# Waits by tile, unread matrix products and an earlier square root in the stages ahead of a recurrence

## The chip, the cores and the metric

The kernel runs on one core of a Trainium2 chip. The metric is the device time of one launch in microseconds (us), as the median of several runs. Beside it there is one profiled execution, whose trace gives every instruction's start and length. Engines are named as the profile names them: PE (matrix products; PEld its weight loads), DVE (vector), ACT (scalar, with function tables), POOL (GpSimd), SP (which issues transfers). SBUF is the on-chip memory, PSUM the eight banks that PE writes.

## What is computed

The input x is one image of 256 by 256 points with 32 channels. Four layers follow each other, and each adds its result to x. `_gn` normalises over the whole image in 16 groups of two channels, so no layer can begin its work on the values before the one ahead has made its last value.

```python
# layer 0; _L0_conv_ref, called with _gn(x)
mn = (m - mu) * rsqrt(var + LN_EPS) * ln_gamma + ln_beta     # over the 32 channels
v = mn @ Wv
g = sigmoid(mn @ Wg)
a = softmax(einsum('bsihc,btihc->bstih', q, k) * C**-0.5, axis=2)
o = g * einsum('bstih,bsihc->bsihc', a, v)
x = x + (o.reshape(B, s, i, H * C) @ Wo + bo)

# layers 1 and 2: 3x3 mean, the two Sobel gradients, their length
x = x + sqrt(grad_x**2 + grad_y**2 + 1e-6)                   # of pooled _gn(x)

# layer 3: two stacked recurrent cells over 256 steps, 256 sequences
x = x + recurrence(_gn(x), W_lat, W_cell, gn_gamma, gn_beta, W_out, ...)
```

In layer 0 the softmax runs over t, but v in the second einsum has the index s. So the weights a sum to one and drop out: o = g * v. Neither q nor k is computed.

## The kernel before

**Layout.** Partition (j, c) holds channel c of column 4*b + j, the free axis holds the 256 rows s, and b = 0..63 are blocks of four columns. `pair(t, k)` is two blocks, 128 x 512 values; k runs over 32 pairs (`NST`). `xa` and `xb` are the two copies of the image, 64 KB per partition each.

**Order.** The front, the Sobel layers and the recurrence are written under a manual schedule: on each engine the instructions run in the order in which the Python code emits them. The attention, the Sobel body and the recurrence emit from lists of (time, operation) that are sorted by their planned time. An engine whose next instruction has to wait holds up everything behind it.

**Load (L147 to L254).** Ten pieces of columns, `nats`, come by two DMAs each on SP's queue: two half pieces, six whole ones, two half ones. Per pair PE turns the data with `transpose` into a PSUM bank `pt` (seven of them), ACT copies it to `xa` (L250), and DVE takes BN_STATS (L251). After the pieces SP issues the constants `kg`, the weights `wone` (W_v, W_g), gamma, beta, the recurrence's norm parameters `gb`, `kt` and `wc`. `busy_here(n)` emits n products of `ident` with itself into a bank `warm` that nobody reads: seven at the start, three after each of the first two pieces. The last ACT instruction is a `table` call, which makes ACT load the table that has the square root.

**Group norm of layer 0 (L266 to L319).** DVE aggregates the statistics (L267), PE averages over the groups (`pm`, L276), DVE makes `less` (minus the mean), `d` and `q`, PE averages again (`pv`, L284), ACT takes the root `gstd`, DVE its reciprocal `scale` and the scaled centring matrix `cen` (L314). `busy_ln(5)` are five unread products ahead of `pm`. Behind `pv` on PE stand four products for the biases (L288), one for the test whether the recurrence's norm is plain (`total_same`, L790), and two that centre the weights (L300); ACT copies the former into `wbias` and scales the latter into `wv4` and `wg4`. `shifted(k)` writes xb = xa + less for pair k, on DVE, but for pair 2, which ACT does (L303). `compare` and `decide` are DVE's part of the test; the flag that they make is read by SP (L750).

**Layer norm (L321 to L397).** For g = 0..7, the groups of four pairs, PE makes 16 centred products of 32 rows (L366) into four banks, ACT squares them (L390), and PE sums the squares over the channels into a variance bank (L347, issued one group late). The variance of group 0 gives `rstds[0]`, that of the others `rstds[1]`. The first is taken inside the loop:

```python
for j, pc in enumerate(pcs):
    if g == EARLY + 1 and j == 1:          # EARLY = 1
        std = deviations()                 # ACT, L357
        nc.vector.reciprocal(rstds[0], std)   # DVE, L380
        for k in range(3):
            rowsets[k] = rows_of(k)        # SP, L328: 4 transfers per pair
        for k in range(5 * J, NST):
            shifted(k)                     # DVE: pairs 20..31
        ...
        for k in range(3):
            scaled(k)                      # L338: xb *= rows; DVE for k=0, POOL else
    nc.scalar.activation(sqs[-1], pc, AF.Square)
```

Pairs 4 to 19 are shifted by a loop that is emitted at g = 0, after that group's products.

**Attention (L399 to L529).** Per pair and half: PE makes g and v (L459), ACT the sigmoid (`sg`, L468), DVE (v + bias) * sg (L472), PE the projection (L485), ACT and POOL the sum into `xa` (L500, L501), DVE BN_STATS (L504). The products of pair k need `scaled(k)`. Pairs from 3 on have their rows transferred and are scaled in between.

**Sobel layer (L543 to L739), run twice.** `shift` is the group norm: aggregate, `busy(before)`, `pm`, `busy(2)`, two constants on ACT, `d`, `q`, `pv`, `busy(after)`; before is 3 and after is 16. `busy` are unread products of `ident` with `kg`. Then per pair: `convert` (ACT), `twos` and `threes` (DVE), `ends` (ACT), `fours`, `smooth` (DVE for pairs 0 and 1, POOL else), `difference` (POOL), `mixed(k, 1)` on the differences and `mixed(k, 0)` on the smoothed rows (PE, L670), `square` of each (ACT, L676), `total` (DVE, L680), `root` (ACT), `residual` and `statistics` (DVE). A mixed product (k, which) takes blocks up to the first of pair k + 1, which only its last part reads. Rows of `dh` and `sh` in the trace are the differences and the smoothed values.

**Pools.** Tiles come from pools. By default a pool that takes over the memory of closed pools waits, at its first use, for everything that was done with them. Only the pool `keep` has `reuse_waits="tile"`, by which each tile waits just for the users of the memory that it lies on.

Of the kernel before, what the change touches and what calls it, by code (L numbers as in the profile page):

```python
# [11 lines left out]
F32 = mybir.dt.float32  # L12
BF16 = mybir.dt.bfloat16
AF = mybir.ActivationFunctionType
ALU = mybir.AluOpType
AX = mybir.AxisListType
PSUM = bass.MemoryType.PSUM
# [6 lines left out]
P = 128  # L24
H = 128
L = 2
D = 256
# [34 lines left out]
def net_kernel(  # L62
# [20 lines left out]
    nc = tc.nc  # L83
# [6 lines left out]
    second = ExitStack()  # L90
# [23 lines left out]
        return t  # L114

    one = eps_tile(1.0, "one")
    wv4 = big2.tile([P, D], F32, name="wv4")
    wg4 = big2.tile([P, D], F32, name="wg4")
    bo4 = per_channel(b_o, "bo4")
    bout4 = per_channel(b_out, "bout4")  # L120

# [60 lines left out]
    def pair(t, k):  # L182
        return t[:, 2 * k : 2 * k + 2, :].rearrange("p b s -> p (b s)")
# [8 lines left out]
    with tc.tile_pool(name="nat", bufs=6, side="right") as natp, tc.tile_pool(  # L192
        name="ps_in", bufs=7, space=PSUM
    ) as ps_in:
        nats = []
        for wl in WIDTHS:
            name, bufs = ("nat", 6) if wl == 32 else ("half", 4)
            nat = natp.tile([P, 2, wl, C], F32, name=name, bufs=bufs)
            nats.append((nat, w0, wl))
            for h in range(2):  # L200
                nc.sync.dma_start(out=nat[:, h], in_=x_nat[:, h, w0 : w0 + wl, :])
            w0 += wl
        nc.sync.dma_start(out=kg, in_=consts[:, 0:2, :])
        for t, v in (
            (wone[0], w_v),
            (wone[1], w_g),
            (gamma, ln_gamma.rearrange("(c o) -> c o", o=1)),
            (beta, ln_beta.rearrange("(c o) -> c o", o=1)),
        ):
            nc.sync.dma_start(out=t, in_=v)  # L210
        count = mp.tile([1, 1], F32, name="count")
        compare, total_same, decide = norm_test(tc, mp, count, gn_gamma, gn_beta)
        nc.sync.dma_start(out=kt, in_=consts[:, 3:NK, :])
        rw = RecurrentWeights(tc, cells, one, w_cell, b_cell)
        reduces, subtractions = rw.centring()
        wgam = []
        for w in wone:
            wgam.append(mp.tile([C, D], F32, name="wgam", bufs=2))
            nc.gpsimd.tensor_scalar(wgam[-1], w, gamma, None, ALU.mult)
        cen4 = mp.tile([C, J, C], F32, name="cen4")  # L220
        nc.gpsimd.tensor_copy(
            cen4, kg[0:C, K_CEN, 0:C].unsqueeze(1).to_broadcast([C, J, C])
        )
        mean_of = mp.tile([P, J], F32, name="mean_of")
        nc.gpsimd.tensor_sub(mean_of, ident[:, 0:P:C], kg[:, K_CEN, 0:P:C])
        nc.gpsimd.memset(avg, 0.0)
        for g in range(GROUPS):
            nc.gpsimd.tensor_copy(avg[:, g, g, :], mean_of)

        warm = ps_in.tile([P, P], F32, name="warm", bufs=1)  # L230

        def busy_here(n):
            for _ in range(n):
                nc.tensor.matmul(warm, lhsT=ident, rhs=ident, start=True, stop=True)

        busy_here(7)
        for i, (nat, w0, wl) in enumerate(nats):
            for b2 in range(wl // (2 * J)):
                pt = ps_in.tile([P, 2, 2, P], F32, name="pt")
                for b in range(2):  # L240
                    for h in range(2):
                        lo = (b2 * 2 + b) * J
                        nc.tensor.transpose(
                            pt[:, b, h, :],
                            nat[:, h, lo : lo + J, :].rearrange("p w c -> p (w c)"),
                            ident,
                        )
                blk = w0 // J + b2 * 2
                dst = xa[:, blk : blk + 2, :].rearrange("p b s -> p (b s)")
                nc.scalar.copy(dst, pt.rearrange("p b h s -> p (b h s)"))  # L250
                nc.vector.bn_stats(stats[:, blk // 2, :], dst)  # L251
            if i < 2:
                busy_here(3)
        table(AF.Sqrt, xa[:, NB - 1, 0:1])  # L254

    big3 = second.enter_context(tc.tile_pool(name="big3", bufs=1, side="right"))
    xb = big3.tile([P, NB, S], F32, name="xb")
    cen = mp.tile([P, P], F32, name="cen")

    psums = ExitStack()  # L260
    ps_at = psums.enter_context(tc.tile_pool(name="ps_at", bufs=1, space=PSUM))

    def bank(n):
        return ps_at.tile([P, 2 * S], F32, name="pa", tag=f"bank{n}")
# [5 lines left out]
    def busy_ln(n):  # L270
        for _ in range(n):
            nc.tensor.matmul(junk[:, 0:S], lhsT=ident, rhs=kg, start=True, stop=True)

    busy_ln(5)
    pm = bank(1)[:, 0:1]
    nc.tensor.matmul(pm, lhsT=kg[:, K_GN, :], rhs=mv[:, 0:1], start=True, stop=True)  # L276
    less = small.tile([P, 1], F32, name="less")
    nc.vector.tensor_scalar_mul(less, pm, -1.0)
    d = small.tile([P, 1], F32, name="d")
# [2 lines left out]
    nc.vector.scalar_tensor_tensor(q, d, d, mv[:, 1:2], ALU.mult, ALU.add)  # L282
    pv = bank(2)[:, 0:1]
    nc.tensor.matmul(pv, lhsT=kg[:, K_GN, :], rhs=q, start=True, stop=True)  # L284
    pbias = bank(3)
    for i, w in enumerate(wone):
        for half in range(2):
            nc.tensor.matmul(  # L288
                pbias[:, 2 * i + half : 2 * i + half + 1],
                lhsT=w[:, half * P : (half + 1) * P],  # L290
                rhs=beta,
                start=True,
                stop=True,
            )
    compare()
    psame = bank(6)[0:1, 0:1]
    total_same(psame)
    pws = [bank(4 + i)[:, 0:D] for i in range(2)]
    for pw, w in zip(pws, wgam):
        nc.tensor.matmul(  # L300
            pw, lhsT=cen4.rearrange("c j k -> c (j k)"), rhs=w, start=True, stop=True
        )
    nc.scalar.activation(pair(xb, 2), pair(xa, 2), AF.Identity, bias=less)  # L303
    gstd = small.tile([P, 1], F32, name="gstd")
    nc.scalar.activation(gstd, pv, AF.Sqrt, bias=gn_eps)

    def shifted(k):
        nc.vector.tensor_scalar(pair(xb, k), pair(xa, k), one, less, ALU.mult, ALU.add)

    shifted(0)  # L310
    shifted(1)
    scale = small.tile([P, 1], F32, name="scale")
    nc.vector.reciprocal(scale, gstd)
    nc.vector.tensor_scalar(cen, kg[:, K_CEN, :], scale, None, ALU.mult)  # L314
    shifted(3)
    decide(psame, flag)
    nc.scalar.copy(wbias, pbias[:, 0:4].rearrange("p (i h) -> p i h", i=2))
    for w, pw in zip((wv4, wg4), pws):
        nc.scalar.activation(w, pw, AF.Copy, scale=scale)  # L319

    EARLY = 1  # L321
    rstds = [lnp.tile([P, 2 * S], F32, name=f"rstd{i}") for i in range(2)]
# [14 lines left out]
        e = nc.gpsimd if k else nc.vector  # L337
        e.tensor_mul(pair(xb, k), pair(xb, k), rowsets.pop(k))  # L338

    with tc.tile_pool(name="lnq", bufs=9) as lnq:  # L340
        pvars = []

        def variance(g, sqs):
# [17 lines left out]
        for g in range(GROUPS):  # L361
# [13 lines left out]
                    shifted(k)  # L375
            sqs = []
            for j, pc in enumerate(pcs):
                if g == EARLY + 1 and j == 1:
                    std = deviations()
                    nc.vector.reciprocal(rstds[0], std)  # L380
                    for k in range(3):
                        rowsets[k] = rows_of(k)
                    for k in range(5 * J, NST):
                        shifted(k)
                    for f in reduces:
                        f()
                    for k in range(3):
                        scaled(k)
                sqs.append(lnq.tile([P, 2 * S], F32, name="sq"))
                nc.scalar.activation(sqs[-1], pc, AF.Square)  # L390
# [46 lines left out]
        (20.2213, "r", 0, 0),  # L437
        (22.5883, "bn", 0, 0),
    ]
    with tc.tile_pool(name="at", bufs=3) as atp:  # L440
        free = [4, 5, 6, 0, 1, 2, 3, 7]
        held, sbuf = {}, {}
        slots = {name: list(range(n)) for name, n in (("sg", 10), ("o", 11))}
# [10 lines left out]
        def one_of(o, u, j, k):  # L454
            bias = lambda i: wbias[:, i, u : u + 1]
            if o in ("v", "g"):
                rows = slice(j * C, (j + 1) * C)
                w = wv4 if o == "v" else wg4
                nc.tensor.matmul(  # L459
                    take((o, u, j, k)),  # L460
                    lhsT=w[rows, u * P : (u + 1) * P],
                    rhs=pair(xb, k)[rows],
                    start=True,
                    stop=True,
# [65 lines left out]
    psums.close()  # L530
    front.close()
    lns.close()
    lw = ctx.enter_context(tc.tile_pool(name="lw", bufs=1))
    rw.rest(tc, lw, ident, bout4, w_lat, b_lat, w_out)


# [6 lines left out]
    def sobel_layer(src, dst, moments, before, after, between):  # L543

        stats = new_stats()
        stack = ExitStack()
        kp = stack.enter_context(tc.tile_pool(name="sobk", bufs=1))
        sp = stack.enter_context(tc.tile_pool(name="sob", bufs=2))
        ps_s = stack.enter_context(tc.tile_pool(name="ps_s", bufs=3, space=PSUM))
        ps_c = stack.enter_context(tc.tile_pool(name="ps_c", bufs=2, space=PSUM))  # L550

        along = [kp.tile([P, RING, S], F32, name="sh"), kp.tile([P, RING, S], F32, name="dh")]

# [184 lines left out]
        stack.close()  # L738
        return stats  # L739

    stats = sobel_layer(xa, xb, stats, 3, 16, [rw.selectors])
    stats = sobel_layer(xb, xa, stats, 3, 16, rw.products())
    second.close()


# [2 lines left out]

    inputs = RecurrentInputs(tc, ctx, xa)
    plain = nc.values_load(flag, min_val=0, max_val=1)  # L750
    with tc.tile_pool(name="ps_n", bufs=1, space=PSUM) as ps_n:
        with tc.manual_schedule():
            gn = group_norm(stats, ps_n, 3, 1, 2)
            table(AF.Sigmoid, gn[0])
            weights = rw.finish(lw, ps_n, gn)
# [571 lines left out]
```

## Time and profile before

| what | us |
|---|---|
| three runs | 2498.34, 2499.75, 2502.77 |
| their median | 2499.75 |
| the profiled execution | 2498.01 |
| its span, first to last instruction | 2496.2 |
| load, to the last copy into `xa` | 0 to 28.86 |
| group norm of layer 0, to the first layer-norm product | 30.35 to 35.46 |
| layer norm, squares | 37.51 to 57.1 |
| attention, first product to the last BN_STATS | 58.15 to 288.6 |
| Sobel layers, from aggregate to aggregate | 288.64, 411.46, 537.48 |
| recurrence, from its first product | 545.03 |

The page's head:

```
span 2496.2 us, 42484 instructions
PE 2452.5 (98%) x11615; PEld 1036.2 (42%) x11615; DVE 2242.0 (90%) x6644; ACT 2243.5 (90%) x6876; POOL 1697.2 (68%) x2371
```

Busy shares are means over stages that are unlike each other, and four fifths of the span are the recurrence. Unread products count as busy PE. So the stages ahead of 545 us have to be read one by one, from the timeline (start, length, engine, line, operation, output<-inputs, shapes; in brackets how long the engine was idle before and what released it) and from the table of busy time by stretches.

### The profile page before, as it was taken

What the parts mean: (1) busy time and instruction counts of PE and PEld (TensorE: products, weight loads), DVE (VectorE), ACT (ScalarE), POOL (GpSimd) and SP (SyncE); (2) the same over time, 40 slices, a digit from 0 to 9 for tenths busy, and PEclk for the clock granted to TensorE, in tenths of its full rate; (3) what the DMA queues carried; (4) which work ended last, traced back from release to release, by engine and by line L of the source; (5) the groups of instructions that cost most, each with busy time, mean ns of one, the idle gap of its engine ahead of it and who ended that gap; (6) DMA issues with size and microseconds to landing.
All of it is one profiled execution on the core that took longest, in us unless ns stands there. A gap on an engine that the chain in (4) does not pass through costs nothing.

```text
span 2496.2 us, 42484 instructions
## 1 busy us (share of the span) xinstructions
PE 2452.5 (98%) x11615; PEld 1036.2 (42%) x11615; DVE 2242.0 (90%) x6644; ACT 2243.5 (90%) x6876; POOL 1697.2 (68%) x2371
## 2 busy tenths in 40 slices
PE   8999999989999999999999999999999999999997
PEld 4333466653433433333343343333334333333332
DVE  7788898968999999999999999999999999999996
ACT  6788676759999999999999999999999999999997
POOL 1443386847777777777777777777777777777775
PEclk9999999989999999999999999999999999999999
DMA  6887000020101010101010000000000001000000
GB/s 176 50 40 39 2 1 1 1 51 1 22 5 22 5 22 5 22 5 22 7 24 9 19 12 16 13 15 17 10 20 8 21 7 22 5 5 6 5 5 11
DMA packets 117564, 46.78 MB, mean 19 GB/s; under 512 B 77010, under 2 KB 110003, under 8 KB 117316
## 3 DMA queue, kind: packets, MB, share of 16 engines
q1 hardware_dynamic: 115940, 43.80, 12.5%
q8 instruction: 95, 1.56, 0.3%
q14 instruction: 153, 1.25, 0.2%
q10 hardware_dynamic: 1088, 0.13, 0.0%
q0 software_dynamic: 288, 0.03, 0.0%
HBM read 10.37 MB, written 8.39 MB: 8 GB/s over the span
## 4 chain that ended last, share of the span: by engine, by line
PE 71%; DVE 4%; ACT 2%; issue 1%; POOL 0%; DVEq 0%; ACTq 0%; POOLq 0%
PE zz L1137 34%; PE zz L1132 15%; PE zz L1105 9%; PE pt L1197 5%; PE zz L1102 3%; PE pt L1193 2%; PE px L1242 1%; ACT ga L1126 1%; PE px L1232 1%; DVE ve L1150 1%; DVE st L1257 1%; DVE c L1189 1%; DVE c L1181 1%; ACT go L1126 0%; ACT th L1200 0%
## 5 line engine op out<-in xcount | busy, mean ns | idle before, releaser
L1154 POOL TENSOR_TENSOR rs<-ve,mhalf 128x2 f32<-128x2 f32 x1024 | 705.7, 689 | 538.5 <-DVE ve L1150 519.8
L1137 PE MATMUL zz<-wc,hT 128*128 128x512 f32 x2040 | 1059.5, 607 | 0.8 <-DVE hT L1203 0.7
L1126 ACT ACTIVATE ga<-zz,rs 128x128 f32<-128x128 f32 x3072 | 961.9, 370 | 7.7 <-POOL rs L1154 7.4
L1173 POOL TENSOR_TENSOR rs<-ve,mhalf 128x2 f32<-128x2 f32 x1024 | 742.2, 725 | 0.0
L1150 DVE TENSOR_REDUCE ve<-sq 128x4 f32<-128x516 f32 x1024 | 703.6, 687 | 21.5 <-ACT sq L1145 9.5
L1145 ACT ACTIVATE sq<-zz 128x512 f32<-128x512 f32 x1024 | 620.7, 606 | 39.8 <-PE zz L1137 16.7
L1132 PE MATMUL zz<-wc,hT 128*128 128x512 f32 x1024 | 525.0, 594 | 0.0
L1137 PEld LDWEIGHTS zz<-wc,hT 128*128 128x128 f32 x2040 | 317.4, 190 | 337.2 <-DVE c L1189 176.5
L1126 ACT ACTIVATE go<-zz,rs 128x128 f32<-128x128 f32 x1024 | 384.9, 376 | 0.3 <-POOL rs L1173 0.3
L1181 DVE TENSOR_TENSOR c<-ga 128x128 f32<-128x128 f32 x1024 | 295.9, 289 | 87.5 <-ACT ga L1126 56.2
L1185 DVE TENSOR_TENSOR fc<-ga,c 128x128 f32<-128x128 f32 x1020 | 295.6, 290 | 3.2 <-ACT ga L1126 3.2
L1189 DVE TENSOR_TENSOR c<-c,fc 128x128 f32<-128x128 f32 x1020 | 286.3, 281 | 8.8
L1105 PE MATMUL zz<-fx,xt 32*128 32x512 f32 x2048 | 266.6, 589 | 0.0
L472 DVE SCALAR_TENSOR_TENSOR o<-pa,wbias,sg 128x512 f32<-128x512 f32 x256 | 177.4, 744 | 29.8 <-ACT sg L468 20.5
L468 ACT ACTIVATE sg<-pa,wbias 128x512 f32<-128x512 f32 x256 | 160.1, 685 | 45.0 <-PE pa L459 40.3
L1197 PEld LDWEIGHTS pt<-ident,c 128*128 128x128 f32 x512 | 71.1, 139 | 293.3 <-DVE c L1189 284.6
L1200 ACT ACTIVATE th<-pt 128x128 f32<-128x128 f32 x512 | 145.4, 284 | 47.7 <-PE pt L1197 19.1
L1193 PEld LDWEIGHTS pt<-ident,go 128*128 128x128 f32 x512 | 71.1, 139 | 264.6 <-ACT go L1126 256.7
L1209 DVE COPY hT<-pt 128x128 f32<-128x128 f32 x512 | 143.6, 281 | 29.1 <-PE pt L1197 28.8
L1132 PEld LDWEIGHTS zz<-wc,hT 128*128 128x128 f32 x1024 | 160.7, 197 | 11.3 <-issue 9.5
L1200 ACT ACTIVATE th<-c 128x128 f32<-128x128 f32 x512 | 161.8, 316 | 0.8 <-DVE c L1189 0.6
L1203 DVE TENSOR_TENSOR hT<-pt,th 128x128 f32<-128x128 f32 x512 | 145.9, 285 | 16.0 <-ACT th L1200 15.8
(194 smaller groups left out, 3050.6 us busy)
## 6 DMA issues: line engine op xcount, KB each, us to landing
xt<-xa SPq DMA_DIRECT2D x256, 64.0 KB, 2.0
rows<-rstd SPq DMA_DIRECT2D x128, 64.0 KB, 6.4
out_dram<-st SPq DMA_DIRECT2D x252, 32.0 KB, 1.7
nat<-in_x_dram SPq DMA_DIRECT2D x12, 512.0 KB, 9.9
half<-in_x_dram SPq DMA_DIRECT2D x8, 256.0 KB, 7.1
wc<-in_L_conv_W_cell_dram SPq DMA_DIRECT2D x2, 512.0 KB, 5.8
kt<-in_consts_dram SPq DMA_DIRECT2D x1, 640.0 KB, 4.4
kg<-in_consts_dram SPq DMA_DIRECT2D x1, 128.0 KB, 7.0
```

What stands on the lines that cost most here:

```text
L1105: nc.tensor.matmul(v["zz", l, h, t], lhsT=inputs.of(t, r), rhs=fx[r, :], start=False, stop=l == 0 and t == 0,)
L1126: nc.scalar.activation(dst, gates(x, g), func, scale=scale)
L1132: nc.tensor.matmul(get("zz"), lhsT=v["hT", 0, t][:, seqs], rhs=wc[:, l, 0, :], start=False, stop=t == 0)
L1137: nc.tensor.matmul(get("zz"), lhsT=v["hT", l, t - 1][:, seqs], rhs=wc[:, l, 1, :], start=False, stop=True,)
L1145: nc.scalar.activation(sqs[l, h, t % 2][:, :, 0:H], four(get("zz")), AF.Square, scale=float(H**-0.5))
L1150: nc.vector.tensor_reduce(ve, sqs[l, h, t % 2], AX.X, ALU.add)
L1154: nc.gpsimd.tensor_tensor(rs[:, now], get("ve")[:, now], inputs.mhalf[:, now], ALU.pow)
L1173: nc.gpsimd.tensor_tensor(get("rs")[:, 2:4], get("ve")[:, 2:4], inputs.mhalf[:, 2:4], ALU.pow)
L1181: nc.vector.tensor_mul(c, gates(get("ga"), 0), gates(get("ga"), 2))
L1185: nc.vector.tensor_mul(fc, gates(get("ga"), 1), get("c"))
L1189: nc.vector.tensor_add(c, c, get("fc"))
L1200: nc.scalar.activation(th, get("pt")[:, 1, 0:P] if turned else get("c"), AF.Tanh)
```

## The change

Five things are changed.

1. **Load.** `busy_here(2)` after every piece instead of three after the first two. Behind the last piece the four bias products are made into the bank `warm`, ACT copies them to `wbias` ahead of its `table` call, and four more unread products follow.
2. **Group norm of layer 0.** `busy_ln(5)` goes. `compare` moves ahead of `pm`, `total_same` and the first weight product right behind `pm`, the second weight product and one unread product behind `pv`. Both weight products go into one bank, and ACT scales them into one tile `wvg` in one instruction, in place of `wv4` and `wg4`. `decide` moves ahead of the shifted pairs. Pairs 2, 3 and 4 are shifted on ACT. The loop over pairs 4 to 19 is not changed, so pair 4 is shifted twice.
3. **Layer norm.** The deviations are taken at j == 0 of group 2, ahead of that group's first square.
4. **Sobel layers.** `after` is 9 instead of 16 in both.
5. **Pools.** `reuse_waits="tile"` for big3, ps_at, lnq, at, lw, sobk, sob, ps_s, ps_c and ps_n.

```diff
-    wv4 = big2.tile([P, D], F32, name="wv4")
-    wg4 = big2.tile([P, D], F32, name="wg4")
+    wvg = big2.tile([P, 2, D], F32, name="wvg")
...
+        def biases():
+            for i, w in enumerate(wone):
+                for half in range(2):
+                    nc.tensor.matmul(
+                        warm[:, P + 2 * i + half : P + 2 * i + half + 1],
+                        lhsT=w[:, half * P : (half + 1) * P],
+                        rhs=beta,
+                        start=True,
+                        stop=True,
+                    )
+            nc.scalar.copy(wbias, warm[:, P : P + 4].rearrange("p (i h) -> p i h", i=2))
...
-            if i < 2:
-                busy_here(3)
+            busy_here(2)
+        biases()
+        busy_here(4)
         table(AF.Sqrt, xa[:, NB - 1, 0:1])
 
-    big3 = second.enter_context(tc.tile_pool(name="big3", bufs=1, side="right"))
+    big3 = second.enter_context(tc.tile_pool(name="big3", bufs=1, side="right", reuse_waits="tile"))
...
-    busy_ln(5)
+    compare()
     pm = bank(1)[:, 0:1]
     nc.tensor.matmul(pm, lhsT=kg[:, K_GN, :], rhs=mv[:, 0:1], start=True, stop=True)
+    psame = bank(6)[0:1, 0:1]
+    total_same(psame)
+    pws = bank(7)
+    products = [
...
+    ]
+    products[0]()
     less = small.tile([P, 1], F32, name="less")
...
     nc.tensor.matmul(pv, lhsT=kg[:, K_GN, :], rhs=q, start=True, stop=True)
-    pbias = bank(3)
-    for i, w in enumerate(wone):
...
-    compare()
-    psame = bank(6)[0:1, 0:1]
-    total_same(psame)
-    pws = [bank(4 + i)[:, 0:D] for i in range(2)]
-    for pw, w in zip(pws, wgam):
...
-    nc.scalar.activation(pair(xb, 2), pair(xa, 2), AF.Identity, bias=less)
+    products[1]()
+    busy_ln(1)
+
+    def shifted(k):
+        if k in (2, 3, 4):
+            nc.scalar.activation(pair(xb, k), pair(xa, k), AF.Identity, bias=less)
+        else:
+            nc.vector.tensor_scalar(pair(xb, k), pair(xa, k), one, less, ALU.mult, ALU.add)
+
+    shifted(2)
     gstd = small.tile([P, 1], F32, name="gstd")
     nc.scalar.activation(gstd, pv, AF.Sqrt, bias=gn_eps)
...
+    decide(psame, flag)
     shifted(0)
     shifted(1)
...
     shifted(3)
-    decide(psame, flag)
-    nc.scalar.copy(wbias, pbias[:, 0:4].rearrange("p (i h) -> p i h", i=2))
-    for w, pw in zip((wv4, wg4), pws):
-        nc.scalar.activation(w, pw, AF.Copy, scale=scale)
+    shifted(4)
+    nc.scalar.activation(wvg, pws.rearrange("p (i d) -> p i d", i=2), AF.Copy, scale=scale)
...
-                if g == EARLY + 1 and j == 1:
+                if g == EARLY + 1 and j == 0:
                     std = deviations()
...
-                w = wv4 if o == "v" else wg4
...
-                    lhsT=w[rows, u * P : (u + 1) * P],
+                    lhsT=wvg[rows, int(o == "g"), u * P : (u + 1) * P],
...
-    stats = sobel_layer(xa, xb, stats, 3, 16, [rw.selectors])
-    stats = sobel_layer(xb, xa, stats, 3, 16, rw.products())
+    stats = sobel_layer(xa, xb, stats, 3, 9, [rw.selectors])
+    stats = sobel_layer(xb, xa, stats, 3, 9, rw.products())
```

## The prediction

> **What bounds the kernel now.** I read first the chain of waits, in order of time. Its columns are start, length, and what ran.
>
> ```profile
> 544.90 0.14 issue
> 545.03 1.55 PE px L1225 x6
> ```
>
> The chain goes back only to 544.90: there the recurrence begins, whose 2496.2 - 544.90 = 1951.3 us the change doesn't touch. What comes before is serial by data (each group norm needs the whole image before it), so a microsecond gained ahead of 544.90 is a microsecond at the end. Next I read the busy time by stretches (PE, PEld, DVE, ACT, POOL, then granted clock, DMA share, GB/s):
>
> ```profile
> 32.00:35.00 3.00, 2.49 (x16) 2.16 (x16) 2.68 (x14) 1.43 (x4) 0.00 (x0) 0.90 0.37 141
> 35.00:37.00 2.00, 2.00 (x34) 0.45 (x33) 2.00 (x6) 0.66 (x2) 0.00 (x0) 0.50 0.05 12
> 62.00:68.00 6.00, 4.42 (x14) 2.36 (x18) 0.33 (x1) 3.12 (x5) 1.26 (x1) 0.50 0.84 47
> 68.00:286.00 218.00, 217.75 (x1522) 77.71 (x1514) 192.87 (x286) 176.45 (x285) 86.43 (x85) 1.00 0.67 36
> 298.30:407.60 109.30, 109.30 (x585) 66.28 (x584) 99.41 (x156) 83.16 (x153) 91.28 (x90) 1.00 0.00 1
> ```
>
> In the attention (68 to 286) and in each Sobel layer's body TensorE has no gap: these stretches keep their length, and what can move is when they begin. The clock is at half around 35 to 41 and 62 to 68. What sets the attention's begin is in the timeline:
>
> ```profile
> 34.97 7.37 DVE L308 TENSOR_SCALAR xb<-xa,one,less 128x512 f32<-128x512 f32 x16
> 35.46 4.63 PE L366 MATMUL pa<-xb,cen 32*32 32x512 f32 x64
> 37.51 4.03 ACT L390 ACTIVATE sq<-pa 128x512 f32<-128x512 f32 x8 [1.47 <-PE pa L366]
> 43.29 0.68 ACT L357 ACTIVATE std<-pa,ln_eps 128x512 f32<-128x512 f32 x1
> 44.01 3.35 DVE L380 RECIPROCAL rstd<-std 128x512 f32<-128x512 f32 x1 [1.67 <-ACT std L357]
> 47.39 28.22 SPq L328 DMA_DIRECT2D rows<-rstd  x21
> 62.27 1.26 POOL L338 TENSOR_TENSOR xb<-xb,rows 128x512 f32<-128x512 f32 x1 [30.66 <-DMA rows<-rstd]
> 63.59 3.96 PE L459 MATMUL pa<-xb,wg 32*128 32x512 f32 x10 [3.46 <-POOL xb L338]
> ```
>
> Backwards: PE waits for the scaled pair 1 (62.27), that for its rows, those for the reciprocal, which ends at 47.36. DVE stood idle 1.67 us before it, waiting for the deviations (43.29), which sit behind nine squares. So the end of that reciprocal, R = 47.36, is the number to follow. The third place is the head of a Sobel layer (the second layer repeats it 122.8 us later):
>
> ```profile
> 291.17 7.15 PE L580 MATMUL pg<-kg,ident 128*128 128x256 f32 x32
> 294.12 1.36 POOL L636 TENSOR_TENSOR dh<-pp 128x512 f32<-128x512 f32 x1 [0.32 <-ACT xp L601]
> 296.66 0.69 DVE L632 TENSOR_TENSOR sh<-v 128x512 f32<-128x512 f32 x1
> 298.25 1.51 PE L670 MATMUL pg<-dh,kt 128*64 128x256 f32 x11
> 298.88 1.04 POOL L636 TENSOR_TENSOR dh<-pp 128x512 f32<-128x512 f32 x1 [3.41 <-DVE pp L620]
> 301.00 1.04 POOL L632 TENSOR_TENSOR sh<-v 128x512 f32<-128x512 f32 x1
> 302.68 0.69 DVE L680 TENSOR_TENSOR ss<-sq,pg 128x512 f32<-128x512 f32 x1 [2.25 <-ACT sq L676]
> ```
>
> The 16 unread products hold PE until 298.3, though the differences for its first real product are there at 295.48.
>
> **Load.** Unread products: 3+3 go, 2 after each of ten pieces and 4 more come, 18 in all. The six before took 0.83 us per three, so two cost 0.55. Before a DMA piece PE idles 0.59 to 0.76, which covers them. The last two halves have no such wait: PE's transposes end at 27.97 + 2 x 0.55 = 29.07, the last copy (0.5) at 29.6. The last BN_STATS starts at 29.64 anyway, since at 0.6 each they trail the copies: cost 0, and at most 0.55 if that cover is gone. The bias products (1.05) follow on PE (0.55 + 1.05, to 30.7), and ACT's new copy of them (0.16) now stands ahead of its table load (1.28), table (0.29), shifted pair 2 (0.72) and gstd (0.26): 30.9, 32.15, 32.45, 33.2, 33.45. The scale on DVE is due at 33.8, after its two shifted pairs, so 0.35 is left: 0.
>
> **Group norm.** Five unread products, the bias products and the second half of L300 leave PE's way to L366. On DVE compare (0.24 + 0.17) moves into the 0.47 in which it waited for pm; decide (0.3) moves ahead of the pairs. q ends at 32.45, decide 32.77, pairs 0 and 1 (1.00) 33.77, scale 33.95, cen 34.3. One wgam product may delay pv by 0.3, inside gstd's slack. Then 15 pairs instead of one and 16 (pairs 3 and 4 go to ACT): 15 x 0.46 = 6.9, DVE free at 41.2. ACT: pairs 3 and 4 to 34.8, the joint wvg 0.7 to 35.5, and pair 4 once more, since the loop over 4..19 still has it: 36.2. Eight squares, 4.03: 40.2.
>
> **Deviations.** They wait for group 0's variance and stand behind eight squares, not nine: 40.2 to 40.9, before DVE is free. So DVE sets R: 41.2 + 3.35 = 44.6, against 47.36: 2.75 earlier. With the clock still at half, L366 (4.63 from 34.4) and four variance products (1.65) give 40.7, deviations 41.4, R = 44.75: 2.6. Squares afterwards, 24 x 0.54, end at 53.9 against 57.1, no longer of account. The twelve row transfers of pairs 0 to 2 move with R, and ahead of them the SP queue holds only the flag's load, which waits for decide, now earlier; no other queue's order changes; pair 1 is scaled from 59.5, pair 2 (68.67 before) from 65.9, and PE from there has no gap. I take 2.6. Bounds: 1.4 (only the deviations' part: 43.29 to about 41.9, when group 0's variance ends) and 3.3 (the squares' whole gain).
>
> The clock: before, it fell at 34.3 though PE was busy 2.73 of the 3 us from 29 to 32 and no gap on PE was longer than 0.94. [...]
>
> **Sobel heads.** Seven of 16 go: 7.15/16 = 0.447 each, 3.1 us. PE is free at 295.2, and mixed products go at 1.35 each (k=0) and 1.72 (k>0; 4 parts of 0.43, and only the last part needs the next pair). (0,1) at 295.2; (0,0) 296.55, its last part at 297.6, after smooth(1) at 297.35; (1,1) at 297.85, last part due 299.15, difference(2) ends 299.92: 0.8 waited; (1,0) 300.4, last part due 301.7, smooth(2) ends 302.04: 0.4 waited; (2,1) 302.5, (2,0) 304.2, (3,1) 305.95. Before, (3,1) began at 307.76: 1.8 gained. Supply follows: the squares of k=0 end 300.2, so DVE's 2.25 idle before L680 goes, threes(4) ends at 304.65 instead of 306.87, POOL's difference(4) at 306.2, due 307.2. From there PE's 3.43 per pair exceeds DVE's 3.35 and POOL's 3.1. Two layers: 3.6. Bounds 2 x 1.4 (PE gains only what smooth(2) allowed before, 0.9 + 0.5) and 2 x 3.1.
>
> **Waits by tile.** They free: the first sg (2.02 idle at 62.57; PE then waits for pair 1 anyhow), L580 at 287.99 (pm needs mv at 289.66), POOL's memsets L556, the lat loads. All off the path: 0. Each scaled pair on POOL gets one more wait, on long finished layer-norm products: a semaphore instruction of 0.043, 31 x 0.043 = 1.3 if it were on the path; POOL is busy 86 of 218 there.
>
> **Sum.** 2.6 + 3.6 = 6.2. The profiled execution took 2498.01 (span 2496.2 plus 1.8 around it); it becomes 2491.8. The median of the runs, 2499.75, lies 1.7 above it: **2493.5**. Bounds: 1.4 + 2.8 = 4.2 and 3.3 + 6.2 = 9.5, so 2490.2 to 2495.5, and 1 us on top for the runs' spread (2498.34 to 2502.77).
>
> **Rivals.** (1) The Sobel gain is lost, because supply and not PE paces the first pairs: only the 2.6 of the front stays, 2497.2, within 0.2%. For: DVE is busy from 290.5 to 300.4. Against: its 2.25 idle follows PE, and PE never pauses later. (2) The front gives nothing, because the load's 18 products land on the path (18 x 0.275 = 5.0, of which 2.6 eat the gain) while the heads give 3.6: 2496.2. For: copies and BN_STATS end within 0.1 of each other. Against: the DMA waits on PE. (3) Slower: at the heads the clock falls. A fall lasted 6.8 us at 34.3 and 61.6, and 17 us at 546; at half clock PE's body, which has no slack, loses half of it, 3.4 to 8.5 per head. From 12.4 us at half clock over both heads on, it eats the 6.2; two long falls give 2499.75 - 6.2 + 17 = 2510.6. For: the fall at 34.3 came without a long gap. Against: PE's largest wait in the new head is 0.8 us. (4) The waits by tile or the wider wvg do nothing: this is in the forecast.
>
> **Chances.** 0.2% is 5 us, about what a measurement of this kernel tells from no change. Forecast (both places pay, 4.2 to 9.5) 0.75; (1) 0.09, (2) 0.07, (3) 0.09. Of the forecast, a few hundredths lie between 4.2 and 5: faster 0.72; same 0.03 + 0.09 + 0.07 = 0.19; slower 0.09. The range reaches up to rival 1, 2498, and down to 2489.5.
>
> **What would show it.** Right: the reciprocal from about 41.2 with DVE idle under 0.3 before it; pair 1 scaled near 59.5; first Sobel product 3 us sooner after its group norm, the third 2 us sooner, with waits of under 1 us; the recurrence from about 538.7. Wrong: bn_aggr after 30.35 by more than 0.3 (load), a clock row below 1.00 between 280 and 530 (rival 3), or PE idle for 2 us after (0,1) (rival 1).

## The result, and the profile after

Fourteen runs of each kernel on one chip: 2493.98 us (median; 2492.88 to 2495.78) for the changed kernel against 2499.82 us (2498.34 to 2503.13) for the kernel before. The ratio is 0.9974, 95% interval 0.9966 to 0.9982: 0.26% faster, 5.8 us. The profiled execution of the changed kernel took 2492.88 us, with a span of 2491.1 (before: 2498.01 and 2496.2).

Where the 5.1 us between the two spans lie, from the starts of the same instructions in both timelines:

| stretch | before | after | gained |
|---|---|---|---|
| start to the first aggregate (load) | 30.35 | 30.11 | 0.24 |
| to the first Sobel aggregate (layers' norms, attention) | 258.29 | 256.03 | 2.26 |
| first Sobel layer | 122.82 | 120.73 | 2.09 |
| second Sobel layer | 126.02 | 123.91 | 2.11 |
| to the recurrence's first product | 7.55 | 7.62 | -0.07 |
| recurrence | 1951.2 | 1952.7 | -1.5 |

The first row is not a gain of the change: over the profiles of all runs below the first aggregate begins at 30.11 to 31.50 us with the new load (nine profiles) and at 30.35 to 31.82 without its 18 unread products (four).

The timeline of the changed kernel's front (start, length, engine, line, operation, output<-inputs, shapes, count, in brackets idle time before and releaser):

```profile
33.75 0.29 DVE L324 TENSOR_SCALAR cen<-kg,scale 128x128 f32<-128x128 f32 x1
33.88 1.22 PE L284 MATMUL pa<-kg,ident 128*128 128x256 f32 x2
33.95 6.93 DVE L314 TENSOR_SCALAR xb<-xa,one,less 128x512 f32<-128x512 f32 x15
35.16 4.44 PE L374 MATMUL pa<-xb,cen 32*32 32x512 f32 x64
37.20 4.03 ACT L398 ACTIVATE sq<-pa 128x512 f32<-128x512 f32 x8 [1.70 <-PE pa L374]
41.05 0.75 ACT L365 ACTIVATE std<-pa,ln_eps 128x512 f32<-128x512 f32 x1
41.83 3.35 DVE L388 RECIPROCAL rstd<-std 128x512 f32<-128x512 f32 x1 [0.96 <-ACT std L365]
60.07 1.26 POOL L346 TENSOR_TENSOR xb<-xb,rows 128x512 f32<-128x512 f32 x1 [28.63 <-DMA rows<-rstd]
```

The deviations now stand behind eight squares, and the reciprocal begins at 41.83, 2.2 sooner; pair 1 is scaled at 60.07 and no longer at 62.27. But DVE is still idle ahead of the reciprocal, 0.96 us: the squares began only at 37.20, since PE's first centred product waited for an unread one (L284), which took 1.22 us at a halved clock and ended 1.1 us after `cen` was ready.

The head of a Sobel layer, same columns:

```profile
288.62 4.13 PE L587 MATMUL pg<-kg,ident 128*128 128x256 f32 x18
292.68 1.51 PE L677 MATMUL pg<-dh,kt 128*64 128x256 f32 x11
297.43 0.64 PE L677 MATMUL pg<-dh,kt 128*64 128x512 f32 x1 [0.23 <-POOL dh L643]
297.80 0.68 DVE L687 TENSOR_TENSOR ss<-sq,pg 128x512 f32<-128x512 f32 x1
299.55 0.64 PE L677 MATMUL pg<-sh,kt 128*64 128x512 f32 x1 [0.18 <-POOL sh L639]
```

The first real product starts 6.54 us after the layer's aggregate (286.14); before, 9.61. PE now waits twice, for difference(2) and smooth(2) on POOL, 0.41 in all. DVE's 2.25 us of idle time ahead of `total` are gone (no bracket at 297.80).

The recurrence's first products, and two rows of the table by stretches (start and end, length, busy PE, PEld, DVE, ACT, POOL, granted clock, DMA share, GB/s):

```profile
538.40 2.90 PE L1232 MATMUL px<-xa,ident 128*128 128x256 f32 x6 [1.59 <-DVE cst L968]
```

```profile
68.00:280.00 212.00, 212.00 (x1489) 75.94 (x1490) 189.32 (x282) 172.54 (x280) 83.90 (x82) 1.00 0.67 36
538.00:545.00 7.00, 5.14 (x12) 2.50 (x12) 1.05 (x4) 0.60 (x1) 0.00 (x0) 0.50 0.40 92
```

The attention is as tight as before and at full clock. The recurrence starts 6.6 us sooner, but at half clock: its six products take 2.90 us and not 1.55. That 1.35 is most of the 1.5 that the recurrence gives back.

### The profile page after: what moved, and what is told of

Read it like the earlier page. It is cut to its first block, busy times and chain, and to the rows that moved or that the text cites. A ratio compares the mean times of both kernels' runs of the same rounds, so it can differ in the third digit from the quotient of the medians.

```text
span 2491.1 us, 42479 instructions
## 1 busy us (share of the span) xinstructions
PE 2451.4 (98%) x11615; PEld 1036.1 (42%) x11615; DVE 2241.1 (90%) x6642; ACT 2244.4 (90%) x6878; POOL 1696.6 (68%) x2371
## 4 chain that ended last, share of the span: by engine, by line
PE 71%; DVE 4%; ACT 2%; issue 1%; POOL 0%; DVEq 0%; ACTq 0%; POOLq 0%
PE zz L1144 34%; PE zz L1139 16%; PE zz L1112 9%; PE pt L1204 5%; PE zz L1109 3%; PE pt L1200 2%; PE px L1249 1%; ACT ga L1133 1%; PE px L1239 1%; DVE ve L1157 1%; DVE st L1264 1%; DVE c L1196 1%; DVE c L1188 1%; ACT go L1133 0%; ACT th L1207 0%
## 5 line engine op out<-in xcount | busy, mean ns | idle before, releaser
L1152 ACT ACTIVATE sq<-zz 128x512 f32<-128x512 f32 x1024 | 620.6, 606 | 41.2 <-PE zz L1144 16.7
L466 PE MATMUL pa<-xb,wvg 32*128 32x512 f32 x1024 | 164.9, 642 | 3.4 <-POOL xb L346 3.4
## 6 DMA issues: line engine op xcount, KB each, us to landing
nat<-in_x_dram SPq DMA_DIRECT2D x12, 512.0 KB, 10.2
```

What stands on the lines that cost most here:

```text
L1152: nc.scalar.activation(sqs[l, h, t % 2][:, :, 0:H], four(get("zz")), AF.Square, scale=float(H**-0.5))
```

## The experiments

All ran in three groups, each group on one chip beside runs of the kernel before (group 1: median 2502.08 of 33 runs; group 2: 2500.65 of 29; group 3: 2502.48 of 25). Besides the time, each profile gives stretches free of scatter elsewhere: R - A, from the first aggregate's start (A) to the end of the first reciprocal of the deviations (R): 17.01 in the kernel before, 15.08 in the changed one; S - A, on to the first Sobel aggregate: 258.29 and 256.03; the two Sobel layers: 122.8, 126.0 and 120.7, 123.9.

**1. The Sobel heads alone.** The kernel before, with

```diff
-sobel_layer(..., 3, 16, ...)
+sobel_layer(..., 3, 9, ...)
```

> The kernel before with 9 instead of 16 unread products in both Sobel heads, nothing else. Theory (the two places add up, and a head is worth what its PE begins earlier less what it then waits): each Sobel layer, from aggregate to aggregate, shortens by 2.1 us as in the changed kernel (122.8 to 120.7 and 126.0 to 123.9), the front up to the first aggregate stays at 288.6, the median lies 4.2 us below before. Rival (the gain of the heads needs the front's change, for instance because the first copies and memsets of a head come earlier through waits by tile): each layer gains under 1.5 us. Rival (the clock): a clock row under 1.00 between 288 and 530 us, and a layer that gets longer.

2497.86 us, ratio 0.9983 [95% interval 0.9974, 0.9992], 4.2 less. Layers 120.78 and 123.93: 2.04 and 2.09 gained, what the changed kernel gains there. R - A stays (16.95).

**2. The deviations' place alone.** The kernel before, with

```diff
-        if g == EARLY + 1 and j == 1:
+        if g == EARLY + 1 and j == 0:
```

> The kernel before with the deviations taken ahead of group 2's first square, nothing else. Theory (the wait of DVE's reciprocal for the deviations is what the front gains from): the deviations start at about 41.9 instead of 43.3, the reciprocal ends at 46.0 instead of 47.36 (DVE's 16 pairs end at 42.34), pair 1 is scaled at 60.9, Sobel's first aggregate at 287.3 instead of 288.64, the median 1.3 us below before. Rival (the front's gain comes from the load and the group norm, and the reciprocal is held by DVE's pairs): the reciprocal ends within 0.4 us of 47.36 and the median stays.

2499.09 us, ratio 0.9987 [0.9978, 0.9996]. R - A 15.90, 1.11 less; S - A 257.03, 1.26 less; the layers unchanged. The stages give what was expected. The median's 3.0 is more than that, and what the excess is comes out under "equal clock" below.

**3. The load's unread products as before.** The changed kernel, with

```diff
+            if i < 2:
+                busy_here(3)
-            busy_here(2)
         biases()
-        busy_here(4)
```

> The changed kernel with the load's unread products as before (three after each of the first two pieces, none after the others, none behind the biases). Theory (the unread products of the load lie in PE's waits and do not hold the clock up, since it fell in the changed kernel too, at 32.5 us): the reciprocal ends within 0.3 us of the changed kernel's 45.18, the time stays within 0.7 us of the changed kernel's 2494.0. Rival (they keep the clock up until 32.5): the clock falls one or more steps of 3.4 us earlier, the transposes take twice as long, the aggregate starts later than 30.4, and 1 us or more is lost.

2497.09 us, ratio 0.998 [0.9971, 0.9989]. R - A 14.98 and S - A 256.25 (changed: 15.08, 256.03), and the first stretch at half clock began 2.5 us after the aggregate, as with the products (2.4). Neither a cost of theirs nor a hold on the clock shows. (The expectations of 3 and 4 set the median beside the changed kernel's first 2494.0; in this group the kernel before is 2.3 slower than there, so the ratio is what can be compared.)

**4. The pools' waits as before.** The changed kernel without `reuse_waits="tile"` on the ten pools.

> The changed kernel with all ten pools waiting as before (only keep waits by tile). Theory (these waits lie off the path): the first sigmoid of the attention waits again until the second reciprocal ends, near 60.4, and its first product of pair 1 starts at the same 61.4; both Sobel layers keep 120.7 and 123.9; the median stays within 0.7 us of 2494.0. Rival (they carry part of the gain of the heads): a Sobel layer is longer by 0.3 us or more.

2496.44 us, ratio 0.9977 [0.9968, 0.9986]. The first sigmoid of the attention waits again as expected (2.02 us idle), and no stage got longer by it. R - A was even shorter, 14.38, in a profile in which the clock fell later; S - A was longer, 257.26, in which it stayed at half for 13.7 us from 59.66.

**5. The changed kernel again, with group 2.**

> The changed kernel itself once more, for a second profile and for its time beside the next three on one chip. Theory (in the first profile the clock fell just ahead of the recurrence, at 537.6, and made its first products take 2.9 instead of 1.55 us; where the windows of the clock lie differs from execution to execution): the stages between the aggregates repeat within 0.2 us in the Sobel layers (120.7, 123.9); the recurrence's length differs by 1 us or more from 1952.7, with the clock's fall at another distance from its start; the front differs by up to 1.5 us with the place of its two falls. Rival (the recurrence is always 1.5 us longer in the changed kernel, because of the change): it stays at 1952.7 within 0.3 us, with the fall again less than 1 us ahead of its first product.

2493.61 us, ratio 0.9973 [0.9963, 0.9982]. R - A 14.98, layers 120.73 and 123.89, the recurrence 1952.9. The expected theory, that the recurrence would differ by 1 us or more, failed here; what came are the numbers of its rival, 1952.7 within 0.3 and the clock's fall (538.79) less than 1 us ahead of the first product (539.47). In experiment 11 it is 1955.2. What the runs show of this fall is in the last section.

**6. Without the unread product ahead of the layer norm.** The changed kernel, with

```diff
-    busy_ln(1)
```

> The changed kernel without the one unread product behind the second weight product in the group norm. Theory (at half clock it stands in the way: in the changed kernel cen was ready at 34.03 and the first layer-norm product began at 35.16, behind the unread one of 1.22 us): the first layer-norm product begins within 0.6 us of cen, the reciprocal ends up to 0.8 us earlier, counted from the first aggregate, that is 14.3 to 14.6 us after it instead of 15.1; the median is 0.3 to 0.8 us below the changed kernel's. Rival (it keeps the clock up): the clock's fall at about 32 to 36 us comes earlier or lasts longer and the reciprocal ends 15.5 us or more after the aggregate.

2494.24 us, ratio 0.9973 [0.9964, 0.9982]: the first centred product 0.14 after `cen` and no longer 1.13, R - A 14.03. In the same profile half clock lasted 17 us from 59.1, and S - A was 257.3: 1.3 longer, though R came a microsecond sooner. The expected 0.3 to 0.8 under the changed kernel's median (2493.61) did not come: it is 0.6 above.

**7. Fewer unread products still.** The changed kernel, with

```diff
-sobel_layer(..., 3, 9, ...)
+sobel_layer(..., 3, 4, ...)
```

> The changed kernel with 4 instead of 9 unread products behind pv in both Sobel heads. Theory (at 9 the supply, not PE, paces the first pairs: the last part of product (1,1) waits for difference(2)): PE begins (0,1) up to 1.4 us earlier, but (1,1)'s last part starts at the same distance from the aggregate, 11.3 us, and the layers stay at 120.7 and 123.9 within 0.15 us; the median stays within 0.7 us of the changed kernel. Rival (more can be gained by fewer): the layers shorten by 0.5 us or more each. Rival (the clock falls in a thinner head): a clock row under 1.00 behind 288 or 408 us and a layer longer by 1 to 3.4 us.

2493.85 us, ratio 0.9977 [0.9968, 0.9986]. Layers 120.74 and 123.92: nothing more. PE's rows of that head, timeline:

```profile
291.83 1.51 PE L677 MATMUL pg<-dh,kt 128*64 128x256 f32 x10 [0.72 <-POOL dh L643]
297.95 0.64 PE L677 MATMUL pg<-dh,kt 128*64 128x512 f32 x1 [0.63 <-POOL dh L643]
300.07 0.64 PE L677 MATMUL pg<-sh,kt 128*64 128x512 f32 x1 [0.18 <-POOL sh L639]
```

The first product comes 5.17 us after the aggregate (286.66), 1.4 sooner than with nine, and the last part of the fourth mixed product at 13.41, exactly as with nine: 299.55 - 286.14. POOL's smooth(2) sets it. The clock did not fall at this head either.

**8. Unread products at the recurrence's door.** The changed kernel, with

```diff
     weights = rw.finish(lw, ps_n, gn)
+    busy(ps_n, 4)
```

> The changed kernel with four unread products behind the last product of the final group norm, where PE idles 1.6 us ahead of the recurrence. Theory (the fall of the clock ahead of the recurrence comes from thin activity in the group norm behind Sobel, and one gap of 1.6 us more or less decides little): the clock falls once between 535 and 552 all the same, for 13.6 to 20.5 us, and the median stays within 0.7 us of the changed kernel. Rival (the gap makes it fall): the fall comes 3.4 us or more later than the recurrence's first product, which takes 1.55 us, and the median is 1 us or more below the changed kernel's.

2493.33 us, ratio 0.9972 [0.9961, 0.9982]. In this profile the clock fell at 546.32, after the first products had run at full clock, and the recurrence took 1951.1, as in the kernel before; in the other profiles of the changed kernel and its variants it took 1952.7 to 1956.2. The products cost 0.5: the recurrence starts 8.12 us after its aggregate, not 7.62. The median is not lower than that of experiment 5, so a gain isn't shown. The expected single fall, and a median near the changed kernel's, came; of the rival, the later fall came and the 1 us did not.

```profile
540.73 1.53 PE L1233 MATMUL px<-xa,ident 128*128 128x256 f32 x6 [0.26 <-PE junk L136]
```

**9, 10, 11. Is the unread product dear, or the clock?** Experiment 6 with pair 4 left to its one shift (9), experiment 6 again (10), the changed kernel a third time (11).

```diff
-                for k in range(J, 5 * J):
+                for k in range(J + 1, 5 * J):
```

> The changed kernel without busy_ln(1), and with pair 4 shifted once (on ACT) instead of twice, so DVE shifts 14 pairs instead of 15 between the centring matrix and the first reciprocal (0.46 less). Theory, front now bound by DVE there: without the unread product the last shift ended 41.71 and the deviations 41.50, so taking a shift away moves the bound to the deviations: the reciprocal's end 13.9 us after the first aggregate (14.03 with 15 shifts; 15.08 in the changed kernel), no more than 0.15 gained over no_ln_product. Rival, DVE alone bounds it: 13.57. Sobel layers 120.7 and 123.9. At equal mean granted clock 0.9 to 1.1 us under the changed kernel; if the clock's low stretches give it back, 0.

> The changed kernel without busy_ln(1) a second time. The first time its median stood 0.6 us above the changed kernel's, but its runs had a lower mean granted clock (0.9902 against 0.9915), and at 1.19 us per 0.001 of clock, the slope fitted over the runs, it lay 0.8 us under it. Theory, the unread product costs 1.0 ahead of the group norm and the clock decides the rest: at equal clock again 0.4 to 1.2 us under the changed kernel, reciprocal's end 14.0 to 14.3 after the first aggregate. Rival, the product is worth its cost because it holds the clock up: at equal clock no difference, and a lower mean clock again.

> The changed kernel a third time, as the mark for the two others of this call. Its median 4.5 to 7.5 us under the kernel before; at equal mean clock 5.6 under it, with 1.2 us per 0.001 of clock.

2497.89 [0.997, 0.9988], 2497.28 [0.9973, 0.9991] and 2496.25 us [0.9966, 0.9986], ratios 0.9979, 0.9982 and 0.9976. The expectation of 9 took pair 4's second shift to be DVE's; it is ACT's (the changed kernel's DVE row has 15 shifts and so has that of 9), so DVE's bound stayed: R - A 14.09, against 14.03 in 6. And the expectation of 10 (R - A 14.0 to 14.3) failed: 14.77. The eleven profiles with the deviations in their new place order by when the clock fell:

| kernel | clock falls, after A | lasts | first centred product after `cen` | R - A |
|---|---|---|---|---|
| 11, changed | 4.30 | 3.4 | 0.14 | 14.04 |
| 4, pools | 4.27 | 3.4 | 0.15 | 14.38 |
| 6, no product | 4.27 | 3.4 | 0.14 | 14.03 |
| 9, no product, pair 4 once | 3.98 | 3.4 | 0.15 | 14.09 |
| changed; 3; 5; 7 | 2.35 to 2.54 | 6.8 | 1.02 to 1.13 | 14.98 to 15.08 |
| 10, no product | 2.06 | 10.2 | 0.15 | 14.77 |
| 8, fill at the end | 2.87 | 10.2 | 0.73 | 15.36 |
| 2, deviations alone | 3.05 | 6.8 | its group norm is the old one | 15.90 |

Rows of experiment 11, the changed kernel itself, timeline:

```profile
33.48 0.70 PE L284 MATMUL pa<-kg,ident 128*128 128x256 f32 x2
33.91 0.29 DVE L324 TENSOR_SCALAR cen<-kg,scale 128x128 f32<-128x128 f32 x1
34.34 4.10 PE L374 MATMUL pa<-xb,cen 32*32 32x512 f32 x64 [0.17 <-DVE cen L324]
36.20 4.03 ACT L398 ACTIVATE sq<-pa 128x512 f32<-128x512 f32 x8 [0.57 <-PE pa L374]
40.96 3.35 DVE L388 RECIPROCAL rstd<-std 128x512 f32<-128x512 f32 x1
```

At full clock the unread product takes 0.70 and is over before `cen` is there; DVE goes into the reciprocal with no idle time, from its last shift. So the product is in the way only where the clock falls under it. Half clock delays R without it too. Experiment 10, timeline (half clock from 32.85 to 43.09):

```profile
34.86 4.62 PE L373 MATMUL pa<-xb,cen 32*32 32x512 f32 x64
39.41 1.94 PE L354 MATMUL pa<-sq,avg 128*32 128x512 f32 x8
42.20 3.35 DVE L387 RECIPROCAL rstd<-std 128x512 f32<-128x512 f32 x1 [0.64 <-ACT std L364]
```

The centred products follow `cen` (34.72) at once, but the variance products take 1.94 us, against 1.07 in the changed kernel's profile, and DVE is idle again.

**Equal clock.** The mean granted clock of each run is known too, to three places, and within one group the time falls with it: a straight line through the runs, with an offset of its own for each kernel, gives 1.17, 1.19 and 1.07 us per 0.001 of clock in the three groups, and leaves a scatter of 1.0 us where the kernel before has 1.7 to 2.3 without it. The offsets against the kernel before, at equal clock (with two standard errors):

| kernel | offset, us | mean clock of its runs (kernel before) |
|---|---|---|
| 1, heads alone | -4.0 +/- 0.7 | 0.9912 (0.9909) |
| 2, deviations alone | -1.6 +/- 0.7 | 0.9917 (0.9909) |
| 3, load as before | -5.2 +/- 0.7 | 0.9905 (0.9909) |
| 4, pools as before | -5.8 +/- 0.7 | 0.9908 (0.9909) |
| 5, changed | -5.6 +/- 0.7 | 0.9915 (0.9903) |
| 6, no product | -6.3 +/- 0.7 | 0.9902 (0.9903) |
| 7, four at the heads | -5.6 +/- 0.7 | 0.9909 (0.9903) |
| 8, fill at the end | -5.3 +/- 0.8 | 0.9919 (0.9903) |
| 9, no product, pair 4 once | -5.6 +/- 0.8 | 0.9903 (0.9906) |
| 10, no product | -5.7 +/- 0.8 | 0.9900 (0.9906) |
| 11, changed | -6.0 +/- 0.8 | 0.9908 (0.9906) |

Experiment 2 falls from -3.0 to the -1.3 that its stages show, within its error. The two parts alone, -4.0 and -1.6, make up nearly all of the whole's -5.6 to -6.0. Of the variants of the changed kernel none is apart from it: 3 to 10 lie between -5.2 and -6.3. So the 0.9 to 1.1 us expected of 9 and the 0.4 to 1.2 expected of 10 at equal clock did not come: both lie 0.3 to 0.4 above 11, within the error. That is what the rival of 10 forecast, with the lower mean clock (0.9900); but that mean differs from 11's by about as much as the changed kernel's own does from group to group (0.9908 against 0.9915), so it isn't shown that the product holds the clock up. The comparison takes away any gain that a variant has by holding the clock up, so for 8, which is meant to do that, the plain ratio counts; that shows no gain either. No version beats the changed kernel by more than the measurement can tell.

## Why the prediction was right, and where a step of it was off

The forecast was 2493.5, from 2.6 at the front and 3.6 at the heads. The runs gave 2493.98, the stages 2.5 and 4.2, and 1.5 that the sum didn't have went the other way. The total is right partly because errors cancel, which is luck.

**Load: right.** The aggregate is not later than without the unread products (the ranges stand under the first table), and in experiment 3 they are worth nothing in either direction, within 0.7 us. Rival 2 is refuted.

**Front: size nearly right, bound half right.** Without the first row of the table, which is scatter, the front gave 2.26 and not 2.6, and R came 2.18 sooner. "DVE sets R: 41.2 + 3.35 = 44.6", with 0.3 us or less of idle time ahead of the reciprocal, is the case of experiment 11: R - A 14.04, where the forecast has 44.6 - 30.35 = 14.25. In the profile of the changed kernel it is 15.08, because the step "L366 (4.63 from 34.4)" failed: the centred product was put right behind `cen`, and the one unread product that the change leaves ahead of it was not costed. It takes 1.22 at half clock, and DVE stands idle 0.96 for what follows from it. That only this product is to blame isn't shown: experiment 10 has 14.77 without it, in a longer stretch of half clock. The forecast allowed for half clock in the products that it counted (2.6 in place of 2.75), and not for this one.

The deviations' place alone is worth 1.1 to 1.3 of the front (experiment 2). The rest of R - A, 15.90 - 15.08 = 0.8, and 1.9 where the clock fell late (14.04), goes by the timelines to the earlier start of the centred products and squares; no run takes these apart. Further on the clock around 60 us decides what is left of it: from the first product of pair 1 to S it is 224.6 to 225.1 us in the nine profiles with 6.8 us of half clock there, and 226.5 to 227.0 in the four with 13.7 or 17.1, the heads-alone kernel among them. So S - A is 1.0 shorter than in the kernel before in experiment 6 (257.3) and 3.5 shorter in experiment 11 (254.82). By the runs, what is left for this part is 5.8 - 4.0 - 1.6 = 0.2, with an error of about 1: not told from nothing.

**Sobel heads: mechanism right, size too small.** Twice 2.1 came in place of twice 1.8. PE is free 6.54 us after the aggregate (forecast: 6.56), and both waits came where they were put, for difference(2) and for smooth(2), released 11.29 and 13.41 after it (forecast: 11.28 and 13.40). Mis-sized was "0.8 waited". By the starts of the same products in both traces, counted from the aggregate, PE is 3.07 us ahead at its first product, 2.63 behind the wait for difference(2) and 2.22 behind that for smooth(2): the waits cost 0.44 and 0.41 (forecast 0.8 and 0.4). The idle times of 0.23 and 0.18 are shorter because the profile's rows overlap (0.59 long at steps of 0.43). The first wait cost less because what it waited with was due later: the last part of (1,1) comes 4.36 us behind the first product in the kernel before (302.61 - 298.25), where the forecast counted 3.95 (299.15 - 295.2). Another 0.15 goes further on, around 320 us, and why stays open. That POOL's supply, not PE, now bounds the head is shown by experiment 7. Rival 1 named that limit, but with nine products PE loses 0.85 us to it and not the whole gain.

**Rival 3, a fall of the clock at the heads: refuted.** In none of the 13 profiles is the clock low anywhere between 250 and 530, not with four unread products either, with PE waiting 0.72 us ahead of its first product. That a largest wait of 0.8 us speaks against a fall was the author's estimate; no run shows what length of wait would bring one. At 32 to 36 short waits did not keep the clock up: it fell in all 13 profiles (at 34.42 in the kernel before, where the forecast read 34.3), and in the changed kernel's with PE busy 3.16 of the 3.41 us before.

**Waits by tile: right, 0** (experiment 4).

**The recurrence: not in the sum.** "1951.3 us the change doesn't touch" holds for the instructions and not for their clock: all the profiles of the changed kernel had the fall at 536 to 539, ahead of the first products, where the kernel before had it at 546. It costs 1.35 at once. With the heads alone it was so too: in experiment 1 the clock fell at 543.25, the first products (543.31) took 2.90, and the recurrence 1954.0. The sum has no term for it.

## What to carry to other kernels

Thinning filler on the critical path paid until the next supplier decided (2.1 us a Sobel layer from 16 unread products to 9, nothing more from 9 to 4); read from the trace when that supplier is done, and the floor is known before the first trial (here 13.41 us after the aggregate, for nine products as for four). A filler that was off the path at full clock was on it at half clock (one unread product: 0.70 us and over before `cen` in experiment 11, 1.22 us and over 1.1 us after `cen` was ready in the changed kernel's profile), so cost each instruction at both. And where runs scatter, fit the time against the mean granted clock (here 1.07 to 1.19 us per 0.001) before a difference of a few microseconds is believed: one part's 3.0 us were 1.6.

## What the runs showed of the hardware

In each of the 13 profiles all falls and rises of the granted clock, over 2.5 ms, lie on a grid, at multiples of 3.4133 us within 0.01 (but for the last rise, which is where the record ends), with an offset against the kernel's start that is another in each (1.74 in the changed kernel's, 0.44 in experiment 11's). In the changed kernel's they are at 32.46, 39.28, 59.77, 66.59, 537.63, 558.11 and 2479.81. Half clock lasted 1, 2, 3, 4, 5 or 6 such windows. All of the 43 rises before 600 us follow a window with PE busy for 91% or more. But not every busy window had a rise behind it: in experiment 6 PE was busy throughout the windows from 62.52, 65.93 and 69.34 us on, and the clock stayed at half behind each. The falls follow no such simple share; the table by stretches, cut along the windows, of the changed kernel and, in the last line, of experiment 8:

```profile
29.05:32.46 3.41, 3.16 (x24) 2.63 (x24) 3.04 (x11) 2.54 (x5) 2.32 (x12) 1.00 1.00 377
32.46:35.87 3.41, 3.35 (x22) 1.54 (x38) 3.20 (x10) 2.74 (x6) 0.00 (x0) 0.50 0.11 41
56.35:59.76 3.41, 1.65 (x4) 0.37 (x2) 2.91 (x1) 3.20 (x5) 0.00 (x0) 1.00 1.00 47
534.22:537.63 3.41, 2.59 (x13) 0.99 (x12) 2.42 (x7) 1.64 (x3) 0.00 (x0) 1.00 0.44 103
536.08:539.49 3.41, 3.41 (x18) 1.83 (x18) 2.42 (x7) 1.61 (x3) 0.00 (x0) 1.00 0.37 84
```

The clock is full in the first, third and fourth, and half right behind each. PE was busy 93%, 48% and 76% of them, while windows with 51% in experiments 1 and 4, at the end of the attention, were followed by full clock. So the falls do not go by the share of PE's busy time in the profile alone; what they go by stays open. The clock of the same kernel fell 2.4 us or 4.3 us after its aggregate, as the grid lay, and with it R moved by 1.0 us. In all 13 profiles the first fall came at the first grid line from 2.06 us on after the first aggregate; lines at 0.56 to 0.89 passed without one.

Ahead of the recurrence it is alike. Ten profiles have a grid line 6.6 to 7.5 us after the last aggregate, just ahead of the first products (7.6), and no unread products added there; in all ten the clock fell at that line. In the kernel before and in experiment 2 the lines lie at 5.5 and 5.8, then at 8.9 and 9.2, and the first products ran at full clock (1.55 and 1.53). Experiment 8 has a line at 6.89, where the changed kernel (6.86) and experiment 5 (6.93) fell; with the unread products PE was busy for the whole window ahead of it, and the clock stayed. So in this one profile the clock held with the fill, for its price of 0.5 us. Whether the shorter heads put the line there, or chance did, two profiles with the old heads cannot tell.
